# W_out's slabs turned on VectorE in squares of 32, with later gate sums, Newton chains on VectorE and earlier gap loads

## The chip, the core and the metric

The kernel runs on one core of a Trainium2 chip. The metric is device time in microseconds (us) of one execution. Before the change three runs took 3053.82, 3054.60 and 3056.66 us (median 3054.6).

## The reference, cut to what matters

One transformer block over `x` of shape (4, 512, 512), in float32. A two-sided decaying sum (WKV) feeds a gated delta-rule attention with 16 key heads and 32 value heads of width 128; a second WKV feeds a feed-forward layer. What the change touches is the end of the attention and its gates:

```
beta = sigmoid(b);  g = -exp(A_log) * softplus(a + dt_bias)     # gates, then cumulative sums of g
k    = k * rsqrt(mean(k*k) + eps)                               # keys' norm (and queries')
h    = core * rsqrt(mean(core*core) + eps)                      # per value head, 128 wide
h    = norm_w * h * silu(z)
out  = einsum('bsf,df->bsd', h, W_out)                          # W_out is (512, 32*128)
x    = x + out
```

TensorE contracts over partitions, so W_out has to stand with its head dimension f on the partitions: each head's slab of 512 x 128 has to be turned to 128 x 512.

## The kernel before, in words

A unit is one batch row b with one key head and its two value heads: 4 x 16 = 64 units. The main loop (L1706) takes steps i = 1 to 66. Step i works on several units at once, each at another stage: the keys of unit i+6 (`K`), queries, values and triangular inverse of unit i (`F`), the chunk recurrence of unit i-1 (`C`), norm and output preparation of unit i-2 (`O`), and the output product of unit i-3 (`W`). A step begins in the trace with the first matmul `ps_w<-vb,inv_t`.

Every instruction is recorded in program order on its engine (the helper at L80, so the profile gives L80 for all). The order is written out by hand: `plan` (L1173) is a list of 22 slots, numbered here 0 to 21, each a list of calls; an engine that waits in one call holds back all its later ones. Nearly all DMAs go through SP's queue in the same order.

Pieces that the change or the prediction touch:

- W_out. `out_start` (L451; slots 13 and 15) loads head h's slab, in the steps of batch 0 only, into a `raw` tile (a pool of 4). `out_turn` (L471; slots 18 and 19) turns it with four 128 x 128 TensorE transposes into a PSUM bank. `out_end` (L478) copies it out on ScalarE and multiplies by `norm_w`. `out_forms` (L492) makes four differences for a seven-product (Strassen-like) output product, on VectorE when i is 2 mod 4, else on GpSimd (`spare`, L447). The result goes to DRAM (`wosc`), and the later batches load it from there.
- The heads. `head_end` (L995) copies the turned, normed heads from PSUM on ScalarE.
- Newton chains. Reciprocal square roots start on VectorE with two integer instructions (`root_start`) and run three Newton rounds: `root` (L577) on GpSimd with 12 small instructions, `root_now` (L584) on VectorE with 9. In the main loop `out_root` (slot 0) and `key_root` (slot 12) use GpSimd. `key_root` is followed by four small GpSimd instructions (`key_factors`: br, nbr, nbe).
- The group solve. Every four units GpSimd solves 32 x 32 triangular blocks in 30 elimination substeps ("sub", tiles `L` and `t`): substeps 1 to 20 in the step with i = 2 mod 4, 21 to 30 in the next one.
- Gaps. `gap_load` (L593) loads decay exponents: `dkd` for keys ahead (slot 18) and `dkt` for the next unit (slot 21); GpSimd masks them in slots 0 and 1, ScalarE takes their exponentials. `inverse_load` (L724; slot 16) loads the solved blocks.
- Gates. In three steps, at 485, 1214 and 1917 us, the gates of the next batch are made: a product, a series on VectorE, sums with TensorE (`gates_sum`, tile `ps_g`), ScalarE and VectorE copies (`gates_keep`), a turn (`gates_turn`, `ps_gt`).
- Closing. At the end of a batch (steps 18, 34, 50) VectorE also runs 11 additions of 128 x 512 (`out_close`). Eight steps of a batch carry a WKV as well ("extra" steps).


Of the kernel before, what the change touches and what calls it, by code (L numbers as in the profile page):

```python
# [9 lines left out]
F32 = mybir.dt.float32  # L10
I32 = mybir.dt.int32
AF = mybir.ActivationFunctionType
ALU = mybir.AluOpType
# [3 lines left out]
P = 128  # L17
# [23 lines left out]
def kernel(  # L41
# [21 lines left out]
    B, S, D = x.shape  # L63
    HV = A_log.shape[0]
    HQ = HV // 2
    HD = norm_w.shape[0]
    KT = D // P
# [15 lines left out]
    V, A, G, T, Q = (InOrder(e) for e in (nc.vector, nc.scalar, nc.gpsimd, nc.tensor, nc.sync))  # L83
    NB = P // BS
    NM = 2 * NC
    NU = B * HQ
# [6 lines left out]
    def bank(tag, name):  # L93
        return pp.tile([P, 512], F32, tag=tag, name=name, bufs=banks[tag])


    ident = const.tile([P, P], F32, name="ident")
# [7 lines left out]
        out=tri_le, in_=tri_le, compare_op=ALU.is_ge, fill=0.0, base=0,  # L105
# [5 lines left out]
        out=tri_gt, in_=tri_gt, compare_op=ALU.is_gt, fill=0.0, base=0,  # L111
# [8 lines left out]
    for i in range(3):  # L120
        t = const.tile([P, NM, P], F32, name=f"inv_t{i}")
        G.memset(t, 0.0)
        inv_t.append(t)
        t = const.tile([P, NM // 2, 3 * BS], F32, name=f"inv_n{i}")
# [7 lines left out]
    nw = const.tile([P, 1], F32, name="nw")  # L132
# [6 lines left out]
    wosc = dram.tile([HQ, P, 8, D // 2], F32, name="wosc")  # L139
# [6 lines left out]
    with ExitStack() as main:  # L146
# [4 lines left out]
        ld = main.enter_context(tc.tile_pool(name="ld", bufs=4))  # L151
# [10 lines left out]
        units = {}  # L162

        def unit(n):

            return (*divmod(n, HQ), units.setdefault(n, {}))
# [32 lines left out]
        scale = const.tile([P, B], F32, name="scale")  # L199
# [240 lines left out]
        SB = {"B11": 0, "B21": 1, "B22": 2, "T1": 3, "T2": 4, "T3": 5, "T4": 6}  # L440
# [4 lines left out]
        D2 = D // 2  # L445

        def spare(i):  # L447

            return V if i % GROUP == 2 else G

        def out_start(n, h):  # L451

            b, hq, u = unit(n)
            if n == NU - 1:
                w = u[f"wo{h}"] = wp.tile([P, D], F32, **WO_LAST[h], name=f"wo_{n}_{h}")
                for i, at in enumerate(((0, 7), (1, 2))[h]):
                    Q.dma_start(out=w[:, i * D2 : (i + 1) * D2], in_=wosc[hq, :, at])
                return
            if h == 0:
                u["wo"] = wp.tile([P, 7, D2], F32, tag="wo", name=f"wo_{n}")  # L460
                if b:
                    Q.dma_start(out=u["wo"], in_=wosc[hq, :, :7])
            if b == 0:
                raw = u[f"woraw{h}"] = ld.tile([P, KT, P], F32, tag="raw", name=f"woraw_{n}_{h}")
                f = (2 * hq + h) * HD
                Q.dma_start(out=raw, in_=W_out[:, f : f + HD].rearrange("(n p) f -> p n f", p=P))


        WO_LAST = ({"tag": "wk", "bufs": 1}, {"tag": "wx", "bufs": 3})

        def out_turn(n, h):  # L471
            b, hq, u = unit(n)
            if b == 0:
                ps = u[f"wops{h}"] = bank("pj", f"ps_wo_{n}_{h}")
                for k in range(KT):
                    T.transpose(ps[:, k * P : (k + 1) * P], u[f"woraw{h}"][:, k, :], ident)

        def out_end(n, h):  # L478
            b, hq, u = unit(n)
            if b:  # L480
                return
            w, ps = u["wo"], u[f"wops{h}"]
            if h == 0:
                u["b12"] = ld.tile([P, D2], F32, tag="raw", name=f"b12_{n}")
                A.activation(w[:, 0], ps[:, :D2], AF.Copy, scale=nw)
                A.activation(u["b12"], ps[:, D2:], AF.Copy, scale=nw)
            else:
                A.activation(
                    w[:, 1:3].rearrange("p i d -> p (i d)"), ps, AF.Copy, scale=nw
                )  # L490

        def out_forms(n):  # L492
            b, hq, u = unit(n)
            if b:
                return
            w, b12, E = u["wo"], u["b12"], spare(n + 2)
            for out_, x_, y_ in (("T1", b12, "B11"), ("T2", "B22", "T1"), ("T3", "B22", b12), ("T4", "B21", "T2")):
                x_, y_ = (w[:, SB[v]] if isinstance(v, str) else v for v in (x_, y_))
                E.tensor_tensor(w[:, SB[out_]], x_, y_, ALU.subtract)
            if B > 1:  # L500
                Q.dma_start(out=wosc[hq, :, :7], in_=w)
                Q.dma_start(out=wosc[hq, :, 7], in_=b12)


        def project(n, r, half, tag="pp"):
# [71 lines left out]
        def root(v, y, t):  # L577
            for _ in range(3):
                G.tensor_tensor(t, y, y, ALU.mult)
                G.tensor_tensor(t, t, v, ALU.mult)  # L580
                G.tensor_scalar(t, t, -0.5, 1.5, ALU.mult, ALU.add)
                G.tensor_tensor(y, y, t, ALU.mult)
# [43 lines left out]
            u["rk"] = u["kroot"][1]  # L626

        def key_root(n):
            root(*units[n]["kroot"])
            key_factors(n)  # L630

        def key_root_now(n):
# [342 lines left out]
            u["oroot"] = root_start(u["ms"].rearrange("p c h -> p (c h)"), 2 * NC, f"o_{n}")  # L975

        def out_root(n):
            root(*units[n]["oroot"])

        def out_scale(n, h):  # L980
            b, hq, u = unit(n)
# [13 lines left out]
        def head_end(n, h):  # L995
            b, hq, u = unit(n)
            if h == 0:
                u["hS"] = u1p.tile([P, 7, S // 2], F32, tag="hT", name=f"hS_{n}")

            at = u["hS"][:, 0:4:3] if h == 0 else u["hS"][:, 1:3]  # L1000
            A.copy(at, u["ps_h"].rearrange("p (t s) -> p t s", t=2))

        def head_forms(n):
            if n == NU - 1:
# [159 lines left out]
        def last_add(b, c):  # L1164
# [7 lines left out]
        K, F, C, O, W = AHEAD, 0, -1, -2, -3  # L1172
# [44 lines left out]

            [(project, F, 0, 0), (turn, F, 2), (tap, F, 3, 0), (taps, F, 3), ("store",), ("wkv", wkv_sum, "n"), (out_start, O, 0), ("gate", gates_series, 2), ("sub", 12, None)],

            [(chunk_t, C, 2), ("gate", gates_sum), (slab_turn, C, 4), (chunk_t_end, C, 2), (silu, F, 3),  # L1220
             (turn_end, F, 2), ("soon", load_slice), ("wkv", wkv_under), ("sub", 13, None)],

            [(project, F, 0, 1), (turn, F, 1), (slab_turn, C, 5), (slab_end, C, 4),
             (chunk_squares, C, 2), (head_forms, O), (out_start, O, 1), ("gate", gates_beta), ("sub", 14, None)],

            [(chunk_r, C, 3), (key_pairs, K), (tap, F, 0, 0), (slab_end, C, 5), (turn_end, F, 1),
             (tap, F, 0, 1), (chunk_r_end, C, 3), (tap, F, 0, 2), (tap, F, 0, 3),
             (chunk_q_end, C, 3), (inverse_load, F + 1), ("gate", gates_keep), ("sub", 15, None)],

            [(z_product, C, 0, 0), ("gate", gates_turn), (turn, F, 3), (key_matrix, K, 0), (silu, F, 0), ("sub", 16, None)],  # L1230

            [(chunk_w, C, 3), (z_product, C, 0, 1), (out_turn, O, 0), (chunk_w_end, C, 3),
             (turn_end, F, 3), (square, F, 0), (key_matrix, K, 1), ("wkv", wkv_over, 0),
             (gap_load, K + 1, "d"), (slab_start, K + 1, 1), ("sub", 17, None)],

            [(z_product, C, 1, 0), (out_turn, O, 1), (out_end, O, 0), (key_blocks, K), ("wkv", wkv_over, 1), ("gate", gates_rows), ("sub", 18, None)],

            [(chunk_t, C, 3), (norms, F, 0), (queries, F), (z_silu, C, 0), (out_end, O, 1),
             (out_forms, O), ("wkv", wkv_end), ("sub", 19, None)],

            [(z_product, C, 1, 1), (chunk_t_end, C, 3), (norms_copy, F, 0), (queries_end, F, 0), (queries_end, F, 1),
             (chunk_squares, C, 3), (gap_load, F + 1, "t"), ("sub", 20, None)],
# [12 lines left out]
        for pool, tag, count, shape in (  # L1255
# [3 lines left out]
            for i in range(count):  # L1259
                t = pool.tile(shape, F32, tag=tag, name=f"lent_{tag}_{i}")  # L1260
# [6 lines left out]
        for pool, tag, shape in ((u1p, "nz", [P, NC, 2, HD]), (u1p, "hT", [P, 7, S // 2])):  # L1267
            t = pool.tile(shape, F32, tag=tag, name=f"lent_{tag}")
# [147 lines left out]
        for cb in range(KT):  # L1416
            w = ws[cb]
# [352 lines left out]
```

## Time and profile before

| | |
|---|---|
| median of 3 runs | 3054.6 us |
| profiled execution, its own time | 3053.92 us |
| span of its instructions | 3052.2 us |
| granted TensorE clock, mean | 0.985 |
| TensorE (PE) busy | 2945.0 us, 96% |
| VectorE (DVE) busy | 2285.3 us, 75% |
| ScalarE (ACT) busy | 1881.6 us, 62% |
| GpSimd (POOL) busy | 1475.2 us, 48% |
| main loop's first step begins at | 140.6 us |

How to read it: a group's row gives count, busy time, mean duration of one instruction in ns, idle time before it and what ended that idle time. Mean durations of matmuls overlap, since they are pipelined; what a matmul costs the next one is the difference of their starts in the timeline. The view of windows gives busy time of each engine in a stretch, the granted clock, and the DMA share.

### The profile page before, as it was taken

To read this page: it belongs to the slowest core of one execution; us is meant where nothing else is said; L and a number is where in the kernel's file an instruction comes from. 1 tells how busy PE (TensorE), PEld (TensorE's weight loads), DVE (VectorE), ACT (ScalarE), POOL (GpSimd) and SP (SyncE) were. 2 spreads that over 40 slices of the span, in tenths; PEclk is the share of its full clock that TensorE was granted. 3 is DMA by queue.
4 is the path that set the end of the run, shared out by engine and by line. 5 is a ranking of instruction groups with operands and counts; after the bars stand their busy time and mean duration, and the time that the engine had idled before them with its cause. 6 is when DMAs were issued, how large, how long until landed. Compare 5 with 4: busy or idle time off the path is not lost.

```text
span 3052.2 us, 60274 instructions
## 1 busy us (share of the span) xinstructions
PE 2945.0 (96%) x20816; PEld 2124.5 (70%) x20816; DVE 2285.3 (75%) x5101; ACT 1881.6 (62%) x5145; POOL 1475.2 (48%) x3249
## 2 busy tenths in 40 slices
PE   7679999999999999999999999999999999999998
PEld 4447677777777677677777776777777677776765
DVE  7858777778767887788766887778876767687654
ACT  3566666666666666666666666666666566656552
POOL 3126463574634556265543646266443525365313
PEclk9789999999999999999999999999999999999999
DMA  5325454454453433234334433333433333433322
GB/s 135 96 83 164 126 152 134 137 167 123 138 164 113 141 94 117 82 92 131 100 105 121 123 94 107 98 117 102 117 107 110 112 97 92 118 107 108 123 81 82
DMA packets 422465, 351.75 MB, mean 115 GB/s; under 512 B 219857, under 2 KB 337617, under 8 KB 421777
## 3 DMA queue, kind: packets, MB, share of 16 engines
q1 hardware_dynamic: 420240, 347.27, 38.4%
q8 instruction: 167, 2.74, 0.4%
q14 instruction: 138, 1.12, 0.1%
q10 hardware_dynamic: 1920, 0.62, 0.1%
HBM read 268.87 MB, written 78.91 MB: 114 GB/s over the span
## 4 chain that ended last, share of the span: by engine, by line
PE 75%; DVE 10%; POOL 5%; ACT 5%; DMA 2%; issue 2%; SPq 0%; POOLq 0%; ACTq 0%; DVEq 0%
PE ps_p L80 23%; PE ps_z L80 12%; PE ps_out L80 11%; PE ps_w L80 4%; PE ps_s L80 4%; DVE y L80 3%; PE ps_o L80 3%; PE ps_st L80 2%; PE ps_j L80 2%; PE ps_kq L80 2%; PE ps_f L80 2%; POOL t L80 2%; POOL L L80 2%; PE ps_v L80 1%; PE ps_i L80 1%
## 5 line engine op out<-in xcount | busy, mean ns | idle before, releaser
L80 PE MATMUL ps_p<-cT,w 128*128 128x512 f32 x2000 | 958.2, 608 | 16.0 <-ACT w L80 13.6
L80 DVE SCALAR_TENSOR_TENSOR y<-ps_p,cw,y 128x511 f32<-128x511 f32 (+2 forms) x768 | 572.3, 746 | 267.2 <-ACT y L80 252.7
L80 PEld LDWEIGHTS ps_p<-cT,w 128*128 128x128 f32 x2000 | 358.5, 193 | 318.3 <-issue 271.9
L80 PE MATMUL ps_z<-w,cT 128*128 128x256 f32 x2048 | 479.1, 381 | 5.1 <-ACT w L80 5.1
L80 PE MATMUL ps_out<-wo,hS 128*128 128x256 f32 (+1 forms) x1780 | 459.7, 392 | 18.1 <-DVE sums L80 10.3
L80 PEld LDWEIGHTS ps_z<-w,cT 128*128 128x128 f32 x2048 | 376.4, 192 | 48.0 <-ACT w L80 5.3
L80 PEld LDWEIGHTS ps_out<-wo,hS 128*128 128x128 f32 x1780 | 312.9, 191 | 65.8 <-issue 10.4
L80 ACT ACT_TABLE_LOAD x153 | 196.3, 1283 | 174.1 <-DVE y L80 151.4
L80 DVE TENSOR_TENSOR x<-x,ps_out 128x512 f32<-128x512 f32 x240 | 163.7, 685 | 145.2 <-PE ps_out L80 145.2
L80 POOL TENSOR_TENSOR rs_t_k<-rs_y_k 128x4 f32<-128x4 f32 x171 | 57.8, 338 | 441.0 <-DVE rs_y_k L80 432.5
L80 POOL TENSOR_TENSOR L<-L,t 128x30 f32<-128x30 f32 (+14 forms) x450 | 246.6, 548 | 34.8
L80 POOL TENSOR_TENSOR t<-L 128x30 f32<-128x30 f32 (+14 forms) x450 | 229.1, 509 | 31.5 <-DMA L<-blocks_m 0.8
L80 DVE SCALAR_TENSOR_TENSOR o<-o,rs_y_o,nz 128x128 f32<-128x128 f32 x512 | 200.1, 451 | 14.2 <-POOL rs_y_o L80 13.9
L80 ACT ACTIVATE y<-ps_p,cw 128x512 f32<-128x512 f32 x256 | 174.0, 680 | 53.3 <-PE ps_p L80 53.1
L80 ACT ACTIVATE junk<-o 128x128 f32<-128x128 f32 x512 | 157.8, 308 | 75.7 <-DVE o L80 66.9
L80 ACT ACTIVATE v<-y 128x512 f32<-128x512 f32 x128 | 80.7, 630 | 198.4 <-DVE y L80 198.3
L80 ACT ACTIVATE qs<-ps_s,eg 128x128 f32<-128x128 f32 x384 | 119.9, 363 | 133.7 <-DVE r L80 109.2
L80 ACT ACTIVATE dkt<-dkt,gsum 128x128 f32<-128x128 f32 x512 | 162.6, 392 | 50.0 <-POOL dkt L80 49.7
L80 ACT ACTIVATE wd<-ps_w,eg 128x128 f32<-128x128 f32 x384 | 118.5, 361 | 82.7 <-PE ps_w L80 82.4
L80 ACT ACTIVATE dkd<-dkd,gsum 128x128 f32<-128x128 f32 x512 | 156.4, 388 | 17.2 <-POOL dkd L80 16.5
L80 PEld LDWEIGHTS ps_o<-w,dkt 128*128 128x128 f32 x1024 | 153.8, 192 | 14.4 <-ACT w L80 2.1
L80 POOL TENSOR_TENSOR rs_t_o<-rs_y_o 128x8 f32<-128x8 f32 x192 | 38.6, 201 | 256.9 <-DVE rs_y_o L80 232.8
(295 smaller groups left out, 5846.9 us busy)
## 6 DMA issues: line engine op xcount, KB each, us to landing
w<-wsc SPq DMA_DIRECT2D x288, 256.0 KB, 5.1
wo<-wosc SPq DMA_DIRECT2D x47, 896.0 KB, 4.9
dkd<-gsc SPq DMA_DIRECT2D x64, 512.0 KB, 4.1
dkt<-gsc SPq DMA_DIRECT2D x64, 512.0 KB, 4.9
wraw<-in_L_attn_W_qkvz_dram SPq DMA_DIRECT2D x96, 256.0 KB, 3.0
wsc<-w SPq DMA_DIRECT2D x90, 256.0 KB, 2.1
wosc<-wo SPq DMA_DIRECT2D x16, 896.0 KB, 3.7
blocks_m<-dkd SPq DMA_DIRECT2D x256, 32.0 KB, 1.8
```

The costliest lines, as they stand in the source:

```text
L80: return lambda *args, **kw: tc.keep_in_program_order(op(*args, **kw))
```

## The change

- `out_start` loads a slab with four DMAs, each 32 partitions, in runs of 32 floats, so that the tile holds the slab cut into squares of 32 x 32, each square where it belongs, but not yet turned.
- `out_turn` turns the squares with VectorE: two instructions of 128 x 256 for head 0, one of 128 x 512 for head 1, straight into `wo`. The TensorE transposes and `out_end` go away; B12 is kept in the place of T3 until `out_forms` overwrites it, and is stored to DRAM only for the last key head.
- `norm_w` moves into `head_end`, as the scale of its copy.
- `key_root` and `out_root` use `root_now` on VectorE in steps with i = 2 mod 4.
- `gap_load(K + 1, "d")` is asked for ahead of `inverse_load`.
- The gates' sums, copies, turn, beta and store move down by one to three slots.

The diff, cut:

```diff
-                raw = u[f"woraw{h}"] = ld.tile([P, KT, P], F32, tag="raw", name=f"woraw_{n}_{h}")
+                raw = u[f"woraw{h}"] = ld.tile([P, D], F32, tag="raw", name=f"woraw_{n}_{h}")
                 f = (2 * hq + h) * HD
-                Q.dma_start(out=raw, in_=W_out[:, f : f + HD].rearrange("(n p) f -> p n f", p=P))
+                for a in range(4):
+                    Q.dma_start(
+                        out=raw[a * 32 : (a + 1) * 32].rearrange("i (m j) -> i m j", j=32),
+                        in_=W_out[:, f + a * 32 : f + (a + 1) * 32].rearrange(
+                            "(m i) j -> i m j", i=32
+                        ),
+                    )
...
         def out_turn(n, h):
             b, hq, u = unit(n)
-            if b == 0:
-                ps = u[f"wops{h}"] = bank("pj", f"ps_wo_{n}_{h}")
-                for k in range(KT):
-                    T.transpose(ps[:, k * P : (k + 1) * P], u[f"woraw{h}"][:, k, :], ident)
-
-        def out_end(n, h):
-            b, hq, u = unit(n)
             if b:
                 return
-            w, ps = u["wo"], u[f"wops{h}"]
+            w, raw = u["wo"], u[f"woraw{h}"]
             if h == 0:
-                u["b12"] = ld.tile([P, D2], F32, tag="raw", name=f"b12_{n}")
-                A.activation(w[:, 0], ps[:, :D2], AF.Copy, scale=nw)
-                A.activation(u["b12"], ps[:, D2:], AF.Copy, scale=nw)
+                V.transpose(out=w[:, SB["B11"]], in_=raw[:, :D2])
+                V.transpose(out=w[:, SB["T3"]], in_=raw[:, D2:])
             else:
-                A.activation(
-                    w[:, 1:3].rearrange("p i d -> p (i d)"), ps, AF.Copy, scale=nw
-                )
+                V.transpose(out=w[:, 1:3].rearrange("p i d -> p (i d)"), in_=raw)
...
+            if n % HQ == (NU - 1) % HQ and B > 1:
+                Q.dma_start(out=wosc[hq, :, 7], in_=w[:, SB["T3"]])
...
-                Q.dma_start(out=wosc[hq, :, 7], in_=b12)
...
-            root(*units[n]["kroot"])
+            (root if spare(n - K) is G else root_now)(*units[n]["kroot"])
...
-            root(*units[n]["oroot"])
+            (root if spare(n - O) is G else root_now)(*units[n]["oroot"])
...
-            A.copy(at, u["ps_h"].rearrange("p (t s) -> p t s", t=2))
+            A.activation(at, u["ps_h"].rearrange("p (t s) -> p t s", t=2), AF.Copy, scale=nw)
```

In `plan`, counted from 0: `gates_sum` from slot 14 to the end of 17, `gates_keep` from 16 to 18, `gates_turn` from 17 to 19, `gates_beta` from 15 to 19, `gates_rows` from 19 to 20; `gap_load(K + 1, "d")` from 18 to 16, ahead of `inverse_load`; `out_end` is gone from 19 and 20.

## The prediction, as it was put on record

> **What bounds the kernel now.** I read the page first, then the lengths of the main loop's steps, then one step of each kind. The page's parts 1 and 2:
>
> ```profile
> PE 2945.0 (96%) x20816; PEld 2124.5 (70%) x20816; DVE 2285.3 (75%) x5101; ACT 1881.6 (62%) x5145; POOL 1475.2 (48%) x3249
> ...
> PE   7679999999999999999999999999999999999998
> ```
>
> PE is the bound: of its 107 us without work over half lie before the fourth slice. From the starts of `ps_w<-vb,inv_t` in PE's timeline I took each step's length. A step of batches 1 to 3 with nothing extra takes 42.34 us, again and again, without a gap on PE. The view of windows, for a step of batch 0 that turns slabs, a step with gates, the plain step, and the two steps that close batch 1 and follow it (columns: PE, PEld, DVE, ACT, POOL busy, clock, DMA share):
>
> ```profile
> 770.90:816.40 45.50, 45.39 (x337) 33.60 (x336) 32.17 (x76) 29.56 (x80) 29.08 (x70) 1.00 0.49 146
> 1214.20:1267.70 53.50, 48.86 (x349) 35.71 (x348) 36.45 (x96) 30.89 (x86) 11.34 (x35) 0.97 0.31 88
> 1567.30:1609.60 42.30, 42.30 (x309) 30.83 (x308) 27.18 (x70) 26.20 (x75) 10.50 (x34) 1.00 0.34 96
> 1652.00:1695.00 43.00, 42.64 (x309) 30.87 (x308) 37.12 (x84) 26.20 (x75) 26.74 (x63) 1.00 0.42 131
> 1695.00:1743.50 48.50, 45.04 (x318) 32.46 (x318) 39.78 (x79) 29.32 (x78) 34.87 (x70) 0.96 0.45 135
> ```
>
> The plain step has no slack on PE, so PE work taken away there is time gained; in the second and fifth rows PE loses time to others. The sum below is made against the profiled execution, 3053.92 us (span 3052.2 plus 1.7 around it), 0.7 below the median of 3054.6.
>
> **1. TensorE's transposes of W_out go: -14.**
>
> ```profile
> 943.11 0.60 PE L80 MATMUL ps_wo<-ident,woraw 128*128 128x128 f32 x4
> 943.55 1.89 PE L80 MATMUL ps_z<-w,cT 128*128 128x256 f32 x8
> ```
>
> From start to start a group of four costs 0.44 us; 2 heads x 16 units x 0.44 = 14.0. (The group's busy time, 19.2 us for all, counts the pipeline's tail and is the upper end.)
>
> **2. VectorE's transposes: +1.** No row of this trace shows one. Per unit they are two of 128x256 and one of 128x512. Cheapest row: a one-input operation of 128x512 at 419 ns (`ek<-k`), so some 0.9 us per unit; dearest: RECIPROCAL at 1720 ns per 128x256, 6.9 us per unit. I take the float32 addition `x<-x,x_again` from SBUF, 682 ns per 128x512, as nearest: 1.4 us. The cover is DVE's idle time: 8.6 us in an extra step of batch 0 (46.1 - 37.5, 724.8 to 770.9). At slots 18 to 21 of that step DVE idles 0.8 us, and the product `dkt` that follows ends at 770.6, while PE's `ps_o` needs it about 3 us later. So 1.4 us fits and 6.9 would not. Behind the transposes on DVE stand `key_matrix`, the reciprocals and `dkt`. The Trainium skill (VectorE: DVE Perf Modes, The three transpose paths) gives 311 ns for 128x128 in bf16; an estimate from it, 8 blocks, is 2.5 us per unit, which also fits, and the sum would stay.
>
> ACT loses three copies per unit (473 + 468 + 688 = 1.6 us, 26 in all) and gains a scale in `head_end` (688 against 581 ns, 128 times: 14 us). ACT is busy 26 of 42 us in the plain step; zero. If that cover failed, it would be those 14.
>
> **3. The slabs' DMAs and SP's order: -4.** Each slab now costs four issues and 2048 runs of 128 bytes. Nearest row: `inverse_load`, 10 DMAs with 1792 runs of 128 bytes (256 in each of four, 128 in each of six), issued from 760.75 and all landed at 767.1. Scaled by runs, 6.4 x 2048 / 1792 = 7.3 us, the second slab, first issued at 758.6, lands by 766, while DVE gets to it between 764.7 and 766.4 or later: at most 1.3 us of waiting, inside DVE's idle time. SP's six extra issues are 2.7 us per unit at its 0.45; it stands idle for longer between `blocks_m` and `wosc` in most steps. On the other side, `out_forms` no longer waits for ACT's copies (POOL waits 3.2 us for `b` in the step at 294), and the `wosc<-b` issue is gone, so `dkt`, queued behind, starts sooner: I put it at 0.4 to 1.2 us against the step's end. That matters in batch 0 before step 10, where ACT waits for the `dkt` mask and PE for `w` behind it: steps 3 to 7 and 9 lose 0.9, 2.2, 1.9, 1.7, 0.9 and 1.6 us against the plain 45.59 plus 0.44 per extra turn. Bounds: +4 (landing later) to -9 (all of it); `gap_load` of `dkd` passing `inverse_load` costs nothing, since the latter lands 6 us before the step's end and is needed 2.5 us into the next.
>
> **4. Newton chains, POOL's side: -12.** POOL in a step with i = 2 mod 4, and what its lateness does one step later (the chain that ended last, 1690 to 1715):
>
> ```profile
> 1311.99 0.20 POOL L80 TENSOR_TENSOR rs_t_o<-rs_y_o 128x8 f32<-128x8 f32 x1 [4.05 <-DVE rs_y_o L80]
> ...
> 1315.10 0.20 POOL L80 TENSOR_TENSOR rs_y_o<-rs_y_o,rs_t_o 128x8 f32<-128x8 f32 x1
> ```
>
> ```profile
> 1698.82 0.65 POOL L L80
> ...
> 1702.54 0.21 POOL rs_y_o L80
> 1702.77 3.54 DVE o L80 x4
> 1706.32 0.61 DVE sums L80
> 1706.97 1.13 PE ps_out L80 x4
> ```
>
> A chain on POOL is 12 x 0.28 = 3.4 us. Substeps run over into the next step, so its `out_root` ends at 7.7 us after the step's start, DVE's `o` waits 2.05 us, and PE waits 3.46 us for `sums`, after which the clock is low. On DVE a chain is 9 x 0.20 = 1.8 us by the start-up's rows:
>
> ```profile
> 141.65 0.16 DVE L80 TENSOR_TENSOR rs_t_k<-rs_y_k 128x4 f32<-128x4 f32 x1
> 141.84 0.16 DVE L80 SCALAR_TENSOR_TENSOR rs_t_k<-rs_t_k,kn 128x4 f32<-128x4 f32 x1
> ...
> 143.22 1.07 DVE L80 SCALAR_TENSOR_TENSOR rs_y_k<-rs_t_k,rs_y_k 128x4 f32<-128x4 f32 x1
> ```
>
> (the last one met a long POOL instruction, so up to 0.9 more). `key_factors` stays on POOL and must wait for the chain, so POOL gains only 3.4 - 1.8 = 1.6 us there; what it gains at `out_root` is lost in the 8.9 us that it then waits for the key. Losses of the steps with i = 3 mod 4, actual length minus 42.34 (45.59 in batch 0) minus 0.44 per WKV turn: 5.2 (19), 5.2 (35), 2.1 (51), 1.35 (23, 39), 0.7 (27, 43), 0.7 (11), in all 17.3. With POOL 1.6 us ahead, the two of 5.2 fall to about 2 and the others nearly vanish: 12. Bounds: 5 and 17.
>
> **5. Newton chains, DVE's side: +6.** Plain steps have gaps that hide 1.8 us: after the first chain 0.97 and 0.95 us before `x<-x,ps_out` and 2.8 before `y`; after the second, `r` ends at 1345.2 instead of 1344.5 and PE's `ps_w` reads it at 1345.3. In steps 18, 34 and 50 the closing fills DVE without a gap from 1673.2 to 1692.6 and PE already waits 0.27 for `r`; there 1.8 us goes to PE: +2 each. Bounds 0 and +10.
>
> **6. Gates later: -8.**
>
> ```profile
> 1249.99 0.46 PE L80 MATMUL ps_g<-sp_y,tri_le 128*128 128x128 f32 x2 [3.28 <-DVE sp_y L80]
> ...
> 1250.73 3.38 PE L80 MATMUL ps_p<-cT,w 128*128 128x512 f32 x4
> ```
>
> The gates' own PE work is 3.59 + 0.74 + 0.14 = 4.5 us, so 53.5 us holds a loss of 6.7: the wait of 3.28, matmuls at a granted clock of 0.67 behind it (window 1249.9 to 1255; 3.38 instead of 1.88 us), and 1.36 for `ps_gt`. The same at 1917 is 6.9, at 485 3.6. Moved, the sums find `sp_y` ready. Next late is `state`, which stands behind the series on DVE and ends at 1250.36 when PE is at `ps_s` by 1248.7: 1.7 us. Then `ps_gt`, now two `z_product` after the sums, waits for a table load of 1.28, `eg` 0.49, `gsum` 0.26 and two DVE copies of 0.29: 1.1 us. With some clock 3.2 stays; 3.5, 3.7 and 1.6 saved. Bounds 0 and -17.
>
> **7. Step 2: -2.** POOL's chain there waits 13.7 us for `qe`, the `dkd` mask stands behind it, ACT waits 3.35, PE 6.6. With the chain on DVE the mask is free, but `dkt` lands as before: 1 to 3 gained.
>
> Sum: -14 + 1 - 4 - 12 + 6 - 8 - 2 = -33: 3021 for a profiled execution, **3022** as a median.
>
> **Rivals.**
> *DVE takes POOL's place.* The reliefs of 4 and 6 come back as waits for DVE, which gets 3.6 us more in every fourth step and 1.4 in batch 0. For it: 37 to 40 us of 43 to 48 busy in the closing steps. Against: 27 to 32 us in most others. Then -14 + 6 + 1 and little else: about 3045. Chance 0.2.
> *Everything lands.* The bounds of 3, 4 and 6 are reached: -14 - 9 - 17 + 3 - 14 - 3 = -54: 3000. Chance 0.1.
> *The slabs land late (slower).* If the landing goes by runs, four times as many make 13.2 us of the median 3.3; the second slab then comes at 771.8 instead of 762, DVE stands 5.4 us or more in slot 19 with everything behind it, and beyond the 2.9 us of slack that (with the clock falling) is some 4 us in each of 16 steps: -33 + 64, 3086. It decides from about 12 us of landing on: then 2.1 us are lost per step, and 16 x 2.1 is the whole gain. Against: `inverse_load` above. The Trainium skill (DMA: Bandwidth & Descriptors, Specifications) speaks for it: line rate needs 512 bytes or more, and less means read-modify-write. Chance 0.08.
> *The transposes run at RECIPROCAL's rate:* 6.9 us per unit, 4 past the slack in eight extra steps, with clock 5.5: -33 + 44, 3066. Chance 0.04.
>
> That the change doesn't do what it says has no chance of its own: which instructions run, and in which order, is fixed by the program.
>
> **Numbers.** The forecast (3010 to 3036) has 0.55. A measurement here can tell 0.2%, 6 us. Range 3002 to 3050: it leaves out the slower rivals and part of the best case. Faster 0.83, within 0.2% 0.05 (parts of the first rival), slower 0.12.
>
> **What would show it.** Right: steps of batch 0 shorter by 0.9 and no `ps_wo`; transposes near 0.35 and 0.68 us on DVE; `o` starting before 6.2 us into steps 19, 35 and 51 and PE's 3.46 us waits gone; gate steps near 50 us, with `ps_s<-state` and `ps_gt` as remaining waits; steps 18, 34 and 50 longer, about 45. Wrong: DVE waiting for DMA `woraw`, plain steps over 42.4, PE waiting for `r` in every fourth step.

## The result, and the profile after

The changed kernel takes 3048.2 us (median of 20 runs, 3039.5 to 3054.3) against 3054.4 us for the kernel before on the same chip (20 runs, 3050.3 to 3058.1): ratio 0.9975, 95% interval 0.9969 to 0.9981. It is faster by some 7 us where 33 were forecast: direction right, size wrong. The time lies at the upper end of the stated range (3002 to 3050) and outside the forecast's own (3010 to 3036). The profiled execution took 3047.72 us, with a span of 3046.0.

The page's busy times and TensorE's row of the 40 slices, as shown of before:

```profile
PE 2931.9 (96%) x20688; PEld 2109.5 (69%) x20688; DVE 2332.2 (77%) x5419; ACT 1867.4 (61%) x5097; POOL 1407.3 (46%) x2889
...
PE   8679999999999999999999999999999999999998
```

TensorE has 13 us less work and its share stays at 96%: of the 13.1 us of work taken away, only 6.2 show in the span. VectorE got 47 us more, GpSimd 68 less. The view of windows for five steps (15, 24, 32, 34, 35; columns: PE, PEld, DVE, ACT, POOL busy, clock, DMA share). The rows of before show the same steps, but for the first, which is step 14 there; before, 14 and 15 took 45.6 us each:

```profile
820.76:865.68 44.92, 44.72 (x329) 32.87 (x328) 30.35 (x74) 30.57 (x81) 21.72 (x59) 1.00 0.54 151
1216.56:1265.77 49.21, 47.20 (x349) 34.97 (x348) 35.48 (x96) 30.97 (x86) 10.75 (x34) 1.00 0.32 88
1564.57:1606.90 42.33, 42.33 (x309) 30.80 (x308) 27.21 (x70) 26.36 (x75) 10.58 (x34) 1.00 0.38 103
1649.24:1696.17 46.93, 44.59 (x309) 32.29 (x308) 43.48 (x103) 26.37 (x75) 26.76 (x46) 0.96 0.41 134
1696.17:1740.07 43.90, 43.49 (x318) 31.61 (x317) 37.85 (x78) 29.75 (x77) 31.25 (x62) 1.00 0.43 130
```

Step 15 of batch 0 fell from 45.6 to 44.9 us (step 14 only to 45.5), the step with gates from 53.5 to 49.2, the plain one stayed at 42.3. The closing step, 34, *rose* from 43.1 to 46.9, with VectorE busy 43.5 of 46.9 us and the clock at 0.96; the step after it fell from 48.4 to 43.9.

Laid out by step (from one start of `ps_w<-vb,inv_t` to the next, difference to before in us, one profiled execution each), the sum shows where the gain went. Steps 3, 4, 5 and 7 carry an x slice of the WKV; the last row holds the steps in which no part was expected to act:

| steps | before | after | slabs alone | Newton alone | gates alone | gap alone |
|---|---|---|---|---|---|---|
| 0 and 1 | 196.4 | +1.4 | +4.0 | +0.9 | +1.5 | +5.4 |
| 2 | 49.9 | -3.4 | -1.2 | -3.6 | 0.0 | -3.5 |
| 3 to 7 | 238.9 | **+9.3** | **+9.2** | -0.8 | -0.2 | +5.8 |
| 8 (gates) | 53.7 | -2.0 | -0.2 | 0.0 | -2.8 | 0.0 |
| 9 to 17 | 410.4 | -2.4 | -5.8 | +0.1 | +3.2 | -0.8 |
| 24, 40 (gates) | 107.3 | -8.9 | -0.2 | +0.2 | -7.2 | -5.0 |
| 18, 34, 50 | 129.2 | **+12.7** | 0.0 | **+14.5** | 0.0 | +0.2 |
| 19, 35, 51 | 141.3 | -11.0 | -1.4 | -11.1 | +1.0 | -0.7 |
| 23, 27, 39, 43 | 176.0 | -4.0 | 0.0 | -3.4 | 0.0 | -3.2 |
| 22, 26, 30, 38, 42, 46 | 254.0 | +3.7 | 0.0 | +4.2 | 0.0 | 0.0 |
| 58 | 41.7 | +3.4 | +0.1 | +2.7 | 0.0 | +0.1 |
| all others | 1253.3 | -5.0 | -5.9 | -4.0 | -1.9 | -0.7 |

A single profile moves by some 5 us where nothing was changed (last row, and steps 0 and 1): steps 62 and 64, for instance, each have two lengths, 48.3 or 50.0 us and some 76 or 78, in profiles of all these kernels. So medians judge a kernel, and the table only says where.

### The profile page after: what moved, and what is told of

The parts are those of the page before. It is cut to its first block, busy times and chain, and to the rows that moved or that the text cites. A ratio compares the mean times of both kernels' runs of the same rounds, so it can differ in the third digit from the quotient of the medians.

```text
span 3046.0 us, 59988 instructions
## 1 busy us (share of the span) xinstructions
PE 2931.9 (96%) x20688; PEld 2109.5 (69%) x20688; DVE 2332.2 (77%) x5419; ACT 1867.4 (61%) x5097; POOL 1407.3 (46%) x2889
## 4 chain that ended last, share of the span: by engine, by line
PE 74%; DVE 13%; ACT 5%; issue 3%; DMA 2%; POOL 2%; SPq 0%; DVEq 0%; ACTq 0%; POOLq 0%
PE ps_p L80 23%; PE ps_out L80 11%; PE ps_z L80 11%; PE ps_s L80 4%; PE ps_w L80 4%; DVE y L80 3%; PE ps_o L80 3%; PE ps_j L80 2%; PE ps_st L80 2%; PE ps_kq L80 2%; PE ps_f L80 2%; PE ps_i L80 2%; PE ps_v L80 1%; PE ps_kk L80 1%; PE ps_h L80 1%
## 5 line engine op out<-in xcount | busy, mean ns | idle before, releaser
L80 POOL TENSOR_TENSOR L<-L,t 128x30 f32<-128x30 f32 (+14 forms) x450 | 254.5, 565 | 34.9
L80 POOL TENSOR_SCALAR_AFFINE_SELECT dkd<-dkd 128x1024 f32<-128x1024 f32 x64 | 73.6, 1151 | 264.7 <-DMA inv_t<-blocks_t 117.9
L80 DVE SCALAR_TENSOR_TENSOR o<-o,rs_y_o,nz 128x128 f32<-128x128 f32 x512 | 189.2, 431 | 2.4 <-POOL rs_y_o L80 2.3
L80 POOL TENSOR_SCALAR_AFFINE_SELECT dkt<-dkt 128x1024 f32<-128x1024 f32 x64 | 70.6, 1104 | 247.2 <-DMA dkt<-gsc 200.3
L80 ACT COPY w<-ps_w 128x256 f32<-128x256 f32 (+1 forms) x346 | 144.5, 428 | 26.2 <-PE ps_w L80 26.2
```

Of the source, the lines that this page charges most:

```text
L80: return lambda *args, **kw: tc.keep_in_program_order(op(*args, **kw))
```

## The experiments

**The four parts alone.** Each is the kernel before with one part of the change.

Slabs alone:

```diff
-        four TensorE transposes, out_end on ScalarE
+        four DMAs of 128-byte runs per slab, V.transpose, norm_w in head_end
```

> Only the way of W_out's slabs is changed (four DMAs of 128-byte runs each, transposes on VectorE, norm weight at the heads' evacuation); Newton chains, gates and the gap's load stand as in the kernel before. Theory SP (the 24 more issues of the slabs' DMAs crowd SyncE's queue at a step's end and make dkt late in the next): steps 3 to 17 sum to about +5 us against the kernel before, as in the changed kernel, steps 4, 7 and 12 are 2 to 4 us longer, dkt lands 2 to 4 us later in 12 and 16; time 3050 to 3060. Rival A (the gap's load, moved ahead of the inverse's load, is what makes them late): steps 3 to 17 sum to about -18 and the time is 3034 to 3040. Rival B (the Newton chains on VectorE, which run in these steps too, lengthen 4, 7 and 12): the same -18, with step 4, 7 and 12 no longer than before.

Measured 3059.0 us (11 runs; ratio 1.0014, 1.0005 to 1.0022): the part that was to bring 17 us (terms 1 to 3) costs 4. (Its profile, 3052.7 us, is the fastest of the 11 runs.) Steps 3 to 17 sum to +3.2, so neither rival holds: it needs no gap load and no Newton chain. Nor was the theory whole: step 12 did not lengthen though `dkt` landed 8.7 us after the step's start instead of 7.0. Two other waits stand in step 7, in PE's timeline:

```profile
453.19 1.13 PE L80 MATMUL ps_out<-wo,hS 128*128 128x256 f32 x4 [0.78 <-DVE sums L80]
461.39 0.66 PE L80 MATMUL ps_x<-ident,raw_x 128*128 128x128 f32 x4 [2.25 <-DVE x L80]
```

Neither stood there before. Both are waits for VectorE to add up an earlier `ps_out`, that is, for a PSUM bank. `bank("pj", ...)` hands out three banks, and the choice is made when the program is built. Which tile got which bank is read from the built program; the traces show only the waits, which fit it. In the program before, the x slice's tile took the bank of the fifth output product (steps 3, 5 and 7) or of a weight slab (step 4); without the slabs' two tiles per unit it takes that of the sixth product, which is added up later, and the fifth product takes the bank of the fourth.

Newton alone:

```diff
-            root(*units[n]["kroot"])   # and the same for oroot
+            (root if spare(n - K) is G else root_now)(*units[n]["kroot"])
```

> Only the Newton chains are moved: on VectorE wherever VectorE is the spare engine's opposite as in the changed kernel; all else is the kernel before. Theory: the gain of about 15 us in steps 19, 35, 51, 23 and 39 is paid back in 18, 34, 50, 22, 38, 58 (about +20), so the time is 3053 to 3061, with 18 near 47 us. The rival, which is the forecast's own term (-12 and +6): 3046 to 3050, 18 at 44 to 45 us, the rest of the loss at 18 having come from the gates that were moved into it.

Measured 3053.0 us (ratio 0.9991, 0.9982 to 1.0000): the theory, at its lower edge. Step 18 takes 47.9 us without any gate moved, so the gates are not to blame for it.

Gates alone:

```diff
-            [(chunk_t, C, 2), ("gate", gates_sum), (slab_turn, C, 4), ...
+            [(z_product, C, 0, 0), (turn, F, 3), (key_matrix, K, 0), (silu, F, 0), ("gate", gates_sum), ...
...        and gates_beta, gates_keep, gates_turn, gates_rows moved as in the change
```

> Only the gates' parts are asked for later. Theory: steps 24 and 40 shorten by 4 to 5 us each and step 8 by about 2, and nothing else moves: 3042 to 3046. Rival: the gates' parts gained only because the slabs' transposes had left TensorE and the Newton chains GpSimd, then 24 and 40 shorten by less than 2 us each: 3050 to 3054. Second rival: the later parts fall into steps 18, 34 and 50 of VectorE's or GpSimd's full load and cost there 1 to 4 us each (then the Newton chains are not to blame for all of 18's loss).

Measured 3046.8 us (ratio 0.9972, 0.9960 to 0.9983), 8.2 less than before and just above the theory's 3046; no rival holds. Steps 24 and 40 fall by 3.6 each; what step 8 gains (2.8), step 9 lost in this profile (2.9).

Gap alone:

```diff
-             (gap_load, K + 1, "d"), (slab_start, K + 1, 1)
+             (slab_start, K + 1, 1)
...
-             (chunk_q_end, C, 3), (inverse_load, F + 1)
+             (chunk_q_end, C, 3), (gap_load, K + 1, "d"), (inverse_load, F + 1)
```

> Only the gap's load is asked for sooner, ahead of the inverse's load. Theory: step 2 shortens by about 3.4 us and nothing else moves: 3050 to 3052. Rival: ahead of the inverse's load it makes inv_t or the other loads of the step's end late, then steps 4, 7 and 12 are 1 to 4 us longer each and the time is 3055 to 3064.

Measured 3049.8 us (ratio 0.9978, 0.9969 to 0.9987). Step 2 as expected (-3.5); not expected were -2.4 and -2.6 in steps 24 and 40, nor the +5.8 of this profile in steps 3 to 7 (3.4 of them in step 6, where PE waits 2.9 us for `w` instead of 0.7, at half clock behind it), which the median does not bear out. Gates and gap shorten the same two steps, by 3.6 and 2.5 alone and 4.4 together. The four parts alone add to -11.1; together they gave about -7.

**SyncE's queue.** The end of step 11 (its last instruction before 682.0) in the timeline of SyncE's queue, after and then before (where step 12 starts at 678.8):

```profile
671.46 3.08 SPq L80 DMA_DIRECT2D woraw<-in_L_attn_W_out_dram  x4
...
675.21 0.62 SPq L80 DMA_DIRECT2D dkd<-gsc  x1
675.88 1.97 SPq L80 DMA_DIRECT2D inv_t<-blocks_t  x4
677.89 4.27 SPq L80 DMA_DIRECT2D inv_n<-blocks_n  x6
...
683.10 1.85 SPq L80 DMA_DIRECT2D blocks_m<-dkd  x4
685.06 0.39 SPq L80 DMA_DIRECT2D wosc<-wo  x1
...
686.04 0.84 SPq L80 DMA_DIRECT2D dkt<-gsc  x1
```

```profile
666.53 0.58 SPq L80 DMA_DIRECT2D woraw<-in_L_attn_W_out_dram  x1
...
678.33 0.34 SPq L80 DMA_DIRECT2D wosc<-wo  x1
...
680.19 1.07 SPq L80 DMA_DIRECT2D dkt<-gsc  x1
```

Four slab issues take 3.1 us where one took 0.6, the queue runs without a break into the next step, and `dkt` is issued 4.1 us after the step's start instead of 1.4. GpSimd's mask, ScalarE's exponentials, its copy of `w` and PE's `ps_p` follow it. Is it the number of issues or the short runs? The kernel before, with each slab in four DMAs of 512-byte runs:

```diff
-                Q.dma_start(out=raw, in_=W_out[:, f : f + HD].rearrange("(n p) f -> p n f", p=P))
+                for a in range(KT):
+                    Q.dma_start(out=raw[:, a, :], in_=W_out[a * P : (a + 1) * P, f : f + HD])
```

> The kernel before with each slab of W_out loaded by four DMAs of 512-byte runs instead of one, TensorE's transposes kept: the number of issues alone. Theory (SyncE pays by the issue, about 0.5 us each): eight issues take 3.9 us instead of 0.9 to 1.2, the inverse's loads and dkt's issue move by 2 to 3 us as in the run with the slabs alone, and steps 4, 5 and 7 are 0 to 2 us longer: 3053 to 3060. Rival (the 128-byte runs make the issues long): four issues of 512-byte runs take about as long as the one, under 1.5 us for eight, and dkt's issue stays where it was.

```profile
677.11 2.06 SPq L80 DMA_DIRECT2D woraw<-in_L_attn_W_out_dram  x4
```

Per slab the median from the start of the first issue to the end of the last is 2.05 us here, 2.24 with 128-byte runs and 0.45 for the single DMA: SyncE pays by the issue. Of the steps behind it, 4 and 5 hardly moved (0.2 and 0.0 us), but 3, 6 and 7 took 1.3, 3.1 and 0.9 us more. In step 6 it is the same wait for `w` as in the profile of the gap alone, so this one profile does not settle what the issues cost. The time, 3064.5 us, is one execution and has no interval.

The changed kernel with the slabs asked for in slots 11 and 12 (the slots of subs 10 and 11; the expectation names them one too high):

```diff
+             (out_start, O, 0), ("wkv", wkv_scan, "n", False), ("gate", gates_series, 1), ("sub", 10, 30)],
...
+             (slab_end, F, 0), (out_start, O, 1), ("wkv", wkv_scan, "n", True), ("sub", 11, None)],
```

> The changed kernel with the two slabs' loads asked for one to three slots sooner (in the slots of subs 11 and 12 instead of 12 and 14), so that their eight issues no longer stand in SyncE's queue right ahead of the inverse's and dkt's loads. Theory SP: dkt's issue moves back to at most 1.5 us after a step's start in steps 4, 8, 12 and 16, steps 4, 12 and 16 lose the 2.6, 2.0 and 1.0 us that they were longer or lacked; step 7's +4 stays (its cause is another); about -5.5 us against the changed kernel, 3041 to 3044. Rival 1: the issues only push other loads out of their place (project's or the chunks' transfers), steps 3 to 17 stay within 1 us in sum: 3047 to 3049. Rival 2: out_forms' wait for VectorE's transposes makes wo and dkt late, then the earlier loads change nothing in steps 4 and 12 either.

Measured 3042.2 us (ratio 0.9956, 0.9944 to 0.9969): the theory, 6 us less than the change. Steps 12 and 16 take 45.5 and 43.2, `dkt` is issued 0.2 and 0.0 us after their start, step 7 keeps its 51.4. Step 4 went the other way, to 52.7: GpSimd's `dkd` mask now stood behind the outputs' chain.

The changed kernel with the gap's load back behind the inverse's:

```diff
-             (chunk_q_end, C, 3), (gap_load, K + 1, "d"), (inverse_load, F + 1)
+             (chunk_q_end, C, 3), (inverse_load, F + 1)
...
+             (gap_load, K + 1, "d"), (slab_start, K + 1, 1), ("gate", gates_keep)
```

> The changed kernel with the gap's load back in its old slot, behind the inverse's loads. Theory (slabs' issues and the gap's load together delay the inverse's loads past their time): steps 12 and 16 go back to 46.0 and 43.2 as in the run with the slabs alone, step 4 to about 49.6; step 2 becomes 3.4 us longer again, 24 and 40 by up to 1 us; the sum is within 2 us of the changed kernel: 3046 to 3051. Rival (the slabs' issues alone are enough): steps 4, 12 and 16 stay as long as in the changed kernel and the time rises by 3 to 5 us: 3051 to 3054.

Measured 3051.4 us (ratio 0.9986, 0.9977 to 0.9995). Steps 4, 12 and 16 (49.7, 46.1, 43.2) as the theory said, but the time is the rival's (3051 to 3054) and step 2 did not lengthen: the Newton chains free that step too. The gap's load ahead is what pushes 12 and 16 over.

And early slabs (the same edit of the plan) on the run with the slabs alone:

> The kernel before with the slabs turned by VectorE and asked for two and three slots sooner, no other part. Theory (SyncE's queue made 4 to 6 us of the loss of the slabs alone, the shift of the PSUM banks the rest): dkt's issue moves back to under 1 us after the step's start and the time falls by 4 to 6 us against the slabs alone, to 3053 to 3055, still none of the 14 us forecast, because the banks' waits of steps 3, 5 and 7 stay. Rival (the queue made all of it): 3038 to 3042. Second rival (the queue matters only with the gap's load ahead): 3058 to 3060.

Measured 3059.6 us (ratio 1.0016, 1.0007 to 1.0025): the second rival. `dkt`'s issue did move (to 0.4 us and less in most steps), and nothing was won. The queue costs some 6 us with the gap's load ahead, and is not why the slabs alone lose.

**The x slice's bank.** The changed kernel, with the x slice's transposes one slot later:

```diff
-             [(out_product, W, 5), (project, K, 1, 0), (slab_turn, F, 2), ("wkv", turn_slice, "x"),
+             [(out_product, W, 5), (project, K, 1, 0), (slab_turn, F, 2),
...
-             (out_add, W, 5), 
+             (out_add, W, 5), ("wkv", turn_slice, "x"),
```

> The changed kernel with one request moved: the x slice's transposes on TensorE are asked for one slot later, behind out_add's sixth sum, so that the build gives their tile a PSUM bank that ScalarE has long freed. Theory of the banks: without the slabs' transposes two tiles fewer pass through the three banks of the pj tag in each unit with b = 0, the choice of banks shifts, and in step 7 the x slice's transposes get the bank of the sixth out product and wait 2.1 us for VectorE to add it up, with the rest of the step behind it; with the request moved the wait goes and step 7 shortens by 4 to 5 us to 46.5 to 47.5: 3042 to 3045 in all. Rival (step 7 is long because dkt or out_forms come late): step 7 stays at about 51: 3047 to 3050.

Measured 3049.4 us (ratio 0.9977, 0.9967 to 0.9986): missed. The wait of `ps_x` is gone from step 7 and another stands in its place, 3 us earlier in the step:

```profile
451.22 3.22 PE L80 MATMUL ps_p<-cT,w 128*128 128x512 f32 x4 [2.33 <-ACT w L80]
```

That fits the late `dkt`, issued 1.9 us into the step instead of 0.7; with the slabs early as well (below) 0.4 us of this wait is left. The same edit on the slabs alone:

> The run with the slabs alone, and the x slice's transposes asked for one slot later so that their tile gets another PSUM bank. Theory (banks): of the 2.9, 1.0, 1.3 and 4.2 us by which steps 3, 4, 5 and 7 were longer with the slabs alone, the waits of the x slice's transposes for VectorE go (2.5, none, 1.4 and 2.3 us) and in step 7 the half clock after it; 0.8 to 1.1 us per step stays where two out products share a bank. Steps 3, 5 and 7 come to 47.3 to 48.5, the sum of 3 to 17 falls from +3.2 to -5 or lower, the time to 3048 to 3053. Rival (SyncE's queue makes dkt late there as well, and the wait goes over to w): steps 3, 5 and 7 stay within 1 us and the time at 3057 to 3060.

Measured 3060.0 us (ratio 1.0013): step 7 went from 51.6 to 48.3 and step 5 from 49.6 to 48.6, but steps 6, 10 and 14 gave 1 to 2 us back each, PE now waits 0.8 us for `w` in each of the four steps, and the time is the rival's. With both repairs:

> The changed kernel with both: the slabs' loads asked for one to three slots sooner and the x slice's transposes one slot later. Theory (two causes stand in steps 3, 4, 5 and 7, the bank and SyncE's queue, and each alone hides behind the other): step 7 falls to 47 to 48.5, step 3 to 47 to 48.5, 12 and 16 stay at 45.5 and 43.2 as with the slabs early; against the run with the slabs early 5 to 8 us less, 3034 to 3038. Rival (a third wait stands there): step 7 stays over 50 and the time at 3040 to 3043.

Measured 3043.0 us (ratio 0.9958, 0.9946 to 0.9971). Step 7 takes 47.8 and step 3 48.4, as the theory said; steps 3 to 7 sum to +2.2 instead of +9.3. The time is the rival's (3040 to 3043), no less than with the early slabs (3042.2): mechanism shown, worth not shown by this pair.

**The Newton chains and the clock.** With only the outputs' chains back on GpSimd:

```diff
-            (root if spare(n - O) is G else root_now)(*units[n]["oroot"])
+            root(*units[n]["oroot"])
```

> The changed kernel with the Newton chains of the outputs back on GpSimd and only those of the keys on VectorE. Theory: the keys' chains on VectorE make both the gain of 19, 35 and 51 and the loss of 18, 34 and 50, which stay within 0.5 us of the changed kernel; the outputs' chains cost 1.1 us in 22 and 38 and 0.3 in 26, 30, 42 and 46, which goes: 3044 to 3047. Rival: the outputs' chains bring part of the gain, and 19 and 35 go up by 1 us or more each: 3048 to 3052.

Measured 3039.1 us (ratio 0.9945, 0.9930 to 0.9960), 9 us less than the change and more than the theory asked. 18, 34, 50 and 19, 35, 51 stay; the 3.7 us in 22 to 46 go, and step 58, not foreseen, loses 3.3. The outputs' chains on VectorE only cost.

Why does step 18 lose 4.1 us, when the keys' chain is 1.8 us of VectorE? VectorE's timeline and PE's:

```profile
979.56 0.16 DVE L80 TENSOR_TENSOR rs_t_k<-rs_y_k 128x4 f32<-128x4 f32 x1
...
981.13 0.16 DVE L80 SCALAR_TENSOR_TENSOR rs_y_k<-rs_t_k,rs_y_k 128x4 f32<-128x4 f32 x1
981.21 0.68 DVE L80 TENSOR_TENSOR sums<-sums 128x512 f32<-128x512 f32 x1
...
984.64 0.60 DVE L80 SCALAR_TENSOR_TENSOR state<-state,eg,ps_st 128x128 f32<-128x128 f32 x2
```

```profile
985.38 0.67 PE L80 MATMUL ps_s<-state,k 128*128 128x256 f32 x2 [2.09 <-DVE state L80]
```

The chain comes to PE as a wait of 2.1 us. The rest is further down VectorE's row, here in step 34, before (the step starts at 1651.96) and after (1649.24):

```profile
1683.28 1.94 DVE L80 TENSOR_TENSOR hS<-hS 128x256 f32<-128x256 f32 x4
...
1686.82 0.59 DVE L80 SCALAR_TENSOR_TENSOR r<-ps_s,nbe,vb 128x128 f32<-128x128 f32 x2
```

```profile
1683.22 3.17 DVE L80 TENSOR_TENSOR hS<-hS 128x256 f32<-128x256 f32 x4
...
1687.99 0.59 DVE L80 SCALAR_TENSOR_TENSOR r<-ps_s,nbe,vb 128x128 f32<-128x128 f32 x2
```

With the chain gone from GpSimd its substeps begin sooner (30.4 us into the step instead of 32.2) and run beside all four `hS`, which take 1.2 us longer. Counted from the start of its step, this second `r` ends 4.1, 3.9 and 3.3 us later than before in steps 18, 34 and 50: chain 1.8, `hS` 1.2, other VectorE instructions the rest.

Behind the wait for `state` the granted clock falls to one half for about 3.4 us (step 18; sixth of the numbers after the length: PEclk):

```profile
985.40:986.40 1.00, 1.00 (x4) 0.92 (x5) 1.00 (x2) 0.97 (x5) 0.92 (x2) 0.85 0.00 0
986.40:987.40 1.00, 1.00 (x6) 0.91 (x6) 0.97 (x3) 1.00 (x4) 0.92 (x2) 0.50 0.00 0
987.40:988.40 1.00, 1.00 (x6) 1.00 (x6) 1.00 (x2) 0.27 (x1) 0.92 (x2) 0.50 0.00 0
988.40:989.40 1.00, 1.00 (x4) 0.82 (x3) 0.96 (x2) 0.00 (x0) 0.84 (x3) 0.50 0.00 0
989.40:991.00 1.60, 1.60 (x10) 1.30 (x9) 1.60 (x3) 0.00 (x0) 1.52 (x2) 0.96 0.00 0
```

Half of 3.4 us is 1.7 us of PE's time, but it is not why the step is long. Step 34 in the changed kernel, at half clock behind the same wait (0.53 from 1682.2 to 1685.8), and with early slabs, at full clock (1.00 from 1675.8 to 1679.2):

```profile
1682.20 0.98 PE L80 MATMUL ps_s<-state,k 128*128 128x256 f32 x2 [1.90 <-DVE state L80]
...
1688.38 0.75 PE L80 MATMUL ps_w<-r,inv_t 128*128 128x128 f32 x4 [0.36 <-DVE r L80]
```

```profile
1675.79 0.67 PE L80 MATMUL ps_s<-state,k 128*128 128x256 f32 x2 [1.90 <-DVE state L80]
...
1681.98 0.75 PE L80 MATMUL ps_w<-r,inv_t 128*128 128x128 f32 x4 [2.03 <-DVE r L80]
```

At full clock PE only waits longer for `r`: the step takes 46.95 us there and 46.93 here. VectorE sets its length.

In step 7 the half clock follows the wait for the bank, and no longer wait comes behind it, as PE's timeline of after shows (four `ps_p` take 1.98 us ahead of it and 3.06 behind it):

```profile
452.10 1.98 PE L80 MATMUL ps_p<-cT,w 128*128 128x512 f32 x4 [0.81 <-ACT w L80]
...
456.66 0.79 PE L80 MATMUL ps_x<-ident,raw_x 128*128 128x128 f32 x4 [2.14 <-DVE x L80]
...
458.10 3.06 PE L80 MATMUL ps_p<-cT,w 128*128 128x512 f32 x4
```

With the outputs' chains on GpSimd a wait of 2.20 us at this place was followed by the full clock, and step 7 took 49.3 us instead of 51.4 (0.8 of which is the wait for `w`).

The test of the clock, ten more TensorE products ahead of the waiting one:

```diff
+            if n % HQ == 1 and n > HQ and c == 3:
+                for k in range(10):
+                    T.matmul(ps[:, k % 2, 0], lhsT=ident, rhs=ident, start=True, stop=True)
             for i in (1, 0):
                 T.matmul(ps[:, i], lhsT=u[f"x{i}"][:, tok], rhs=u["state"], start=True, stop=True)
```

> The changed kernel with ten more TensorE products of 128x128, about 1.1 us, ahead of the last chunk's products with the state in every sixteenth unit, into the bank that these then overwrite: TensorE works through part of its wait for VectorE in steps 18, 34 and 50. Theory (a wait of about 2 us halves the granted clock for the next 3 to 4 us, which costs 2.2 us more): the wait in 18 and 34 falls to about 1 us, ends at the same time, and the matmuls behind it run at their full rate, so that both steps shorten by about 2.2 us to 44.9 and 44.7; 50 falls only if its second wait stays short: 3042 to 3046. Rival (the slow matmuls have another cause, or the clock follows other idle time): 18 and 34 stay at 46.9 to 47.2 or lengthen by up to 1.1 us: 3047 to 3052.

```profile
984.65 2.47 PE L80 MATMUL ps_s<-ident 128*128 128x128 f32 x20 [2.18 <-DVE state L80]
986.96 0.60 PE L80 MATMUL ps_s<-state,k 128*128 128x256 f32 x2
```

Measured 3046.2 us (ratio 0.9965, 0.9953 to 0.9977); steps 18 and 34 stay at 47.2 and 47.0, the rival's numbers, but the test failed as a test: the added products waited for the same release and cost 2.3 us instead of 1.1. The clock stayed full in all three steps this time, in 18 and 34 after a wait as long as before, and the two steps are as long as at half clock. So a wait of this length does not always bring the half clock, and there it is not what lengthens them. Step 50, the same 2.03 us wait, in the changed kernel and with early slabs (3.4 us behind the wait):

```profile
2384.50:2387.90 3.40, 3.40 (x13) 2.79 (x14) 3.36 (x9) 2.36 (x8) 3.04 (x5) 0.66 0.00 0
```

```profile
2378.50:2381.90 3.40, 3.40 (x18) 3.06 (x19) 3.36 (x9) 2.34 (x8) 3.08 (x5) 1.00 0.00 0
```

13 matmuls against 18 in the same time, and step 50 takes 47.9 against 46.4: here, behind the step's last wait, the half clock costs 1.5 us.

**Do the losses add up?** Three kernels more, of edits shown above: the change with early slabs and with the outputs' chains on GpSimd; the kernel before with the keys' chains, the gates and the gap of the change, so without its slabs; and the change with all three repairs (early slabs, outputs' chains on GpSimd, x slice later). In this order:

> The changed kernel with the slabs' loads asked for two and three slots sooner and the outputs' Newton chains back on GpSimd. Theory: the two losses are at different places (steps 12 and 16 on SyncE's queue; 22, 38 and 58 on VectorE) and their gains of 6.0 and 9.1 us add up: 3032 to 3036. Rival (both runs owe their gain to the same waits of step 3 to 7, or to the clock's dice): 3038 to 3042.

> The kernel before with the keys' chains on VectorE, the later gates and the gap asked for sooner, and W_out's slabs turned by TensorE as before: the whole change but the slabs (and the outputs' chains). Theory: the slabs as changed bring nothing net, their gain of 0.8 us a step in 8 to 17 being spent in 2 to 7 and on SyncE's queue, so that this kernel stands within 3 us of the same kernel with slabs: 3037 to 3043. Rival 1 (they cost, as alone, some 4 us): 3033 to 3036. Rival 2 (beside the other parts they gain as forecast): 3047 to 3056.

> The changed kernel with the slabs' loads asked for two and three slots sooner, the outputs' Newton chains back on GpSimd and the x slice's transposes asked for one slot later. Theory: steps 3 and 7 lose the waits for the bank as in the run with the first and the third of these (1.0 and 3.6 us less), and with the half clock gone behind them the time falls below the run with the first two: 3030 to 3034. Rival (the request's own price, 0.8 us of wait for w in each of steps 3, 4, 5 and 7, and other waits take it up, as the medians of the earlier pair say): 3036 to 3039.

Measured: 3037.0 us (ratio 0.9939, 0.9926 to 0.9951), between theory and rival; 3039.0 (0.9946, 0.9934 to 0.9959), the theory: with the slabs as changed (3039.1) or without them the time is the same (in the two profiles, which differ by the slabs alone, the slabs cost 9.0 us in steps 3 to 7 and bring 6.1 in 9 to 17); and **3032.5** (0.9930, 0.9918 to 0.9942), the theory and the fastest kernel of all, 22 us under before and 16 under the change. There steps 3 to 7 stand at +4.6 instead of +9, steps 9 to 17 at -7.6. The x slice's move is worth 4.5 us here (3037.0 to 3032.5), and the repaired slabs 6.5 us against the kernel without slabs, but the intervals overlap in both pairs.

## Why the prediction was right or wrong

**Terms 1 and 3, the slabs (-14 and -4): this is the step that failed most**, by about 21 us. The work went as costed: with the slabs alone, steps 10, 11 and 13 to 17 are 0.6 to 0.9 us shorter each. The failure is the sentence that PE work taken away "is time gained", carried from the plain step to the early steps of batch 0, and the view that SP "stands idle for longer". Steps 3 to 7 were to give 4.4 us and cost 9.3. The runs showed two causes in these steps, whose shares in the total are not settled (with the slabs alone neither repair by itself gained, 3059.6 and 3060.0 us, and both together were not run there): the x slice's transposes got a bank that VectorE frees late, and the slabs' issues with the gap's load ahead push `dkt` back. I had seen neither: the banks because removing a TensorE operation looked free of side effects, the queue because I priced landing and not the place behind. In the company of the other parts the slabs are worth nothing (3039.1 against 3039.0).

**Term 2 (VectorE's transposes, +1): right.** The group's row of after:

```profile
L80 DVE STREAM_TRANSPOSE wo<-woraw 128x256 f32<-128x256 f32 (+1 forms) x48 | 23.1, 508 | 0.2 <-DMA woraw<-in_L_attn_W_out_dram 0.2
```

0.42 us for 128x256 and 0.68 for 128x512, 1.5 us per unit where 1.4 was taken; VectorE waited 0.2 us in all for a slab. Both slower rivals that hung on it fell: a whole slab landed a median of 4.8 us after its first issue (longest 8.9), later than the 3.3 (6.7) of before, but short of the 12 us from which it was to decide. DMAs of 64 KB landed in a median of 2.8 us with 128-byte runs and 2.1 with 512-byte runs (the run with four issues). The Trainium skill's rule that line rate needs 512 bytes or more (DMA: Bandwidth & Descriptors, Specifications), which spoke for "the slabs land late", agrees with these 0.7 us in direction; a fourfold landing does not show.

**Term 4 (GpSimd's side, -12): right**, -11.0 in 19, 35, 51 and -4.0 in 23, 27, 39, 43. In step 35 the outputs' chain now ends 3.6 us into the step, not 7.7, `o` starts at 5.6, and of PE's wait 0.41 is left:

```profile
1699.61 0.20 POOL L80 TENSOR_TENSOR rs_y_o<-rs_y_o,rs_t_o 128x8 f32<-128x8 f32 x1
```

```profile
1710.89 1.13 PE L80 MATMUL ps_out<-wo,hS 128*128 128x256 f32 x4 [0.41 <-DVE x L80]
```

**Term 5 (VectorE's side, +6): mechanism right, size wrong**, +19.8: the second step that failed, by about 14 us. In 18, 34 and 50 it forecast +2 each, the chain's 1.8 us. VectorE's second `r` came 3.3 to 4.1 us later, and the steps grew by as much. Mis-sized was what VectorE runs beside GpSimd: the sum has nothing for the four `hS`, which took 1.9 us in step 34 of before, beside small instructions of GpSimd. The same trace shows them longer beside its substeps (step 26):

```profile
1340.17 3.12 DVE L80 TENSOR_TENSOR hS<-hS 128x256 f32<-128x256 f32 x4
```

The half clock, which the forecast had read off step 35 of before, added 1.5 us in step 50 and nothing in 18 and 34. And "plain steps have gaps that hide 1.8 us" was wrong for 22 and 38 (+1.1 each, PE waiting for `qe`) and for 58. "DVE takes POOL's place" gave 3045 and came nearest in time, but by luck: the reliefs of terms 4 and 6, which it has come back as waits, did not, and most of the miss is the slabs. ("Everything lands" takes -14 for term 6, whose own bound was -17; nothing hangs on it.)

**Term 6 (gates, -8): right**, 8.2 alone, with the remaining waits as foreseen:

```profile
1252.14 0.67 PE L80 MATMUL ps_s<-state,k 128*128 128x256 f32 x2 [0.87 <-DVE state L80]
...
1262.01 0.30 PE L80 MATMUL ps_gt<-ident,sp_f 128*128 128x128 f32 x1 [1.14 <-DVE beta L80]
```

**Term 7 (step 2, -2): right**, if a little more than its 1 to 3 (-3.4); the gap's load does as much alone. That load, priced at nothing, is worth 5 alone, partly in the gates' steps, and costs some 2 to 3 us in 12 and 16 through the queue once the slabs are there.

## What to carry to other kernels

Work taken off the bounding engine is time gained only in the steps where that engine waits for nothing; and taking an operation away also takes its buffer out of the rotation, so look at who gets which bank afterwards. What an instruction costs depends on what runs beside it on the other engine; work moved from GpSimd to VectorE lets GpSimd's next work start sooner, so read VectorE's times from a stretch where that work already runs beside it. A wait of 2 us on TensorE may cost up to 1.7 us more by the clock (steps 7 and 50 here), or nothing more where a later wait takes it up (18 and 34). Where two waits stand one behind the other, a repair of one can show nothing, because the next takes its place (3049.4 us with the x slice moved, against 3048.2).

## What the runs showed of the hardware

- In the main loop of all 18 profiles, up to step 57, none of TensorE's 148 waits of 1.0 to 1.6 us that began at full clock was followed within 3 us by a granted clock of one half, 53 of the 103 of 1.6 to 2.6 us were, and 83 of the 84 longer ones (2.03 us: both). The half clock lasted 3.4 us or a multiple of it. The Trainium skill (TensorE: Matmul & The Clock Gate, What's actually happening) has half clock after an idle window of about 3.4 us, and full clock after as long a busy one, in a window that runs freely. The 3.4 us of recovery agree; the idle time that was enough is shorter here, and the free-running window would explain why the same wait falls on either side. That such throws of 2 us make the scatter of 15 us among the changed kernel's runs was not tested.
- One `hS` instruction on VectorE (TENSOR_TENSOR, float32, 128x256) took 0.42 us with no substep of GpSimd beside it and mostly 0.7 to 0.9 with one (step 46 of before: four in 1.7 us; steps 18 and 34 of after: four in 3.2). What GpSimd takes from VectorE there was not tested.
- SyncE's queue pays 0.4 to 0.5 us per DMA issue: medians of 0.45 us for one DMA of 512-byte runs per slab, 0.43 for four, and 0.49 for four of 128-byte runs.
